# Two graph-attention layers on one core: layer 1 sums its ones column with the rows and lets a tile's projection run on into the next tile; the first part computes its score columns apart from the weights

## Chip, core and metric

The kernel runs on one core of a Trainium2 chip. The time is the device time of that core in microseconds (us), from the first to the last instruction. Three runs of the kernel before took 2431.86, 2438.90 and 2444.07 us; the median, 2438.9 us, is the number to compare with. The profile was taken in a run of 2431.86 us, and its span is 2430.1 us.

## What is computed

`x` has 3327 rows of 1024 floats, `adj` is a symmetric 0/1 matrix (int32) with ones on the diagonal and about 17 ones per row. Cut to its core, the reference is:

```python
def layer0(x):                       # 8 heads of 128
    h = (x @ W0).reshape(C, 8, 128)
    e = leaky_relu(src(h)[:, i] + dst(h)[:, j], 0.2)      # per head
    attn = softmax(where(adj, e, -inf)); out = attn @ h
    return out
def layer1(x):                       # one head
    h = x @ W1
    e = leaky_relu(h @ a1 + (h @ a2).T, 0.2)
    return relu(softmax(where(adj > 0, e, -9e15)) @ h)
x = layernorm(x + layer0(x))
x = layernorm(x + layer1(x))
```

Everything is float32 on the chip, except where a mask or a bf16 split is named.

## The kernel before

The 3327 rows are 26 tiles of 128 (`NT = 26`). The kernel has three stages, one after the other.

**First part.** For each tile: load 128 rows of `x` and of `adj`, transpose `x`, project it with `W0`, store the projected row with its score terms in device memory (`h0_d`), and turn the tile's mask into a list of edges. A tile of 128 targets has room for `EB = 5` blocks of 512 edges, and each edge has the number of the row to fetch (`idx`) and a one-hot of its target (`oh`). The score columns (8 heads, source and target) are 16 more columns beside `W0`, so one set of products gives both:

```python
ph = Phase(own, "proj", {"A": 2, "S": 1, "T": 2})          # PSUM tags and their buffers
def project(t, ht, cuts):
    for c in cuts:                                          # CUTS0 = (0, 347, 694, 1040)
        c0, c1 = CUTS0[c], CUTS0[c + 1]
        acc = bank("A", [P, c1 - c0], "mm")
        for k in range(KT):                                 # KT = 8
            nc.tensor.matmul(acc, xT[t][:, k, :], wt[:, k, c0:c1], start=k == 0, stop=k == KT - 1)
            if k % 2 == 1:
                fill()                                      # a piece of the edge list of an earlier tile
        m = min(c1, D) - c0
        nc.scalar.activation(ht[:, c0 : c0 + m], acc[:, :m], AF.Copy)
        if c == 2:
            nc.scalar.activation(sd0[:, t]..., acc[:, m:], AF.Copy)
            ...                                             # two small exponentials, then the store of ht
for k in range(KT):                                         # score columns of W0, once
    for n, av in enumerate(avs):
        pr = ph.sbuf("pr", [P, D], 4)
        (nc.vector, nc.gpsimd)[n].tensor_tensor(pr, wt[:, k, :D], av, OP.mult)
        nc.vector.tensor_reduce(wt[:, k, D + n * H : D + (n + 1) * H], ..., AX.X, OP.add)
```

Inside the edge list, a 0/1 matrix `place` sends entries to slots:

```python
nc.vector.scalar_tensor_tensor(mid, off, 1.0, end, op0=OP.mult, op1=OP.add)
nc.scalar.activation(away, self.io_q, AF.Abs, bias=mid, scale=-1.0)
...
nc.vector.tensor_scalar(place, away, deg, None, op0=OP.is_lt)
yield
xp = bank("S", [P, NG, HALF], "xp")                         # four PSUM banks at once
for b in range(EB):
    ...                                                     # 16 small products
    yield
nc.scalar.activation(oh..., xb[:, :, :, :GT], AF.Copy)      # three evictions for all four groups
...
```

**Layer 0.** For each tile, five steps gather 4 x 128 rows of `h0_d` by `idx` and sum them with weights per head. The change does not touch it.

**Layer 1.** For each tile `t`, five steps `b` gather 4 x 128 rows of `y_d` (1024 values, a one, two exponentials), build the weights `es` on VectorE, and sum on TensorE. Four products of 32 output rows each (`g = 0..3`) stand side by side in the array. The sum of the weights is a column of its own (`den`). When the tile is summed it is divided by `den`, transposed and multiplied with `W1`; that projection is a generator (`project1`) whose pieces are called by `fill()` during the next tile's steps:

```python
ph = Phase(own, "sparse", {"A": 4, "S": 2, "T": 1, "D": 1})
def project1(t, z, res):
    xT = sbuf("xT", [P, KT, P], 2)
    yield from ph.transposed(xT, z)          # two pieces: four transposes into tag "T", one copy out
    acc = [bank("S", [P, HALF], "mm") for _ in range(2)]
    for k in range(KT):
        for g in range(2):
            nc.tensor.matmul(acc[g], xT[:, k, :], wt[:, k, g * HALF : (g + 1) * HALF], ...)
        yield
    o = sbuf("z", [P, D], 3, "o")
    for g in range(2):
        nc.scalar.activation(o[:, g * HALF : (g + 1) * HALF], acc[g], AF.Relu)
    nc.vector.tensor_tensor(o, o, res, OP.add)
    ph.layer_norm([o])
    nc.sync.dma_start(out[...], o[:n])
    yield
# class Target:
def begin(self):
    self.acc = [bank("A", [P, HALF], "acc1") for _ in range(2)]
    self.den = bank("D", [P, 1], "den1")
def step(self, b):
    s = self.src.pop(b)
    nc.vector.tensor_tensor(es, R, s[:, :, D + 1 : D + 2], OP.mult)      # cut: broadcasts
    nc.vector.tensor_tensor(es, es, s[:, :, D + 2 : D + 3], OP.max)
    nc.vector.tensor_tensor(es, es, self.oh[:, b * NG : (b + 1) * NG, :], OP.mult)
    for c in range(3):
        for g in range(NG):
            to = self.den if c == 2 else self.acc[c]
            nc.tensor.matmul(to[g * GT : (g + 1) * GT, :], es[:, g, :],
                             s[:, g, c * HALF : min((c + 1) * HALF, D + 1)], start=b == 0, stop=b == EB - 1)
        if c < 2:
            fill()
def finish(self):
    nc.vector.reciprocal(ri[:, :1], self.den)
    nc.scalar.activation(z[:, :HALF], self.acc[0], AF.Copy, scale=ri[:, :1])
    nc.vector.tensor_scalar(z[:, HALF:], self.acc[1], ri[:, :1], None, op0=OP.mult)
    ...
    later.append(project1(self.t, z, res))
for t, tg in enumerate(targets):
    tg.begin()
    for b in range(EB):
        tg.step(b)
        ...                                  # fetch of the same step of the next tile
    while later:
        fill()
    tg.finish()
```

The order in the program is not the order on an engine: the tile framework's scheduler places the instructions of each engine itself when the kernel is built.

Of the kernel before, what the change touches and what calls it, by code (L numbers as in the profile page):

```python
# [26 lines left out]
def kernel(  # L27
# [48 lines left out]
    CUTS0 = (0, 347, 694, HW0)  # L76
# [58 lines left out]
    class Phase:  # L135
# [61 lines left out]
        def iota(self, shape, pattern, name, mult=0, base=0):  # L197

            raw = self.pool.tile(shape, I32, tag="iota", bufs=1, name="iota")
            nc.gpsimd.iota(raw, pattern=pattern, base=base, channel_multiplier=mult)  # L200
            dst = self.pool.tile(shape, F32, bufs=1, name=name)
            nc.vector.tensor_copy(dst, raw)
            return dst

        def edge_constants(self):
# [7 lines left out]
            self.io_q = self.iota([P, EB * P], [[2, EB * P]], "io_q", base=1)  # L213
# [17 lines left out]
        def edges(self, t, words, got):  # L231
# [32 lines left out]

            mid = sbuf("mid", [P, 1], 1)
            nc.vector.scalar_tensor_tensor(mid, off, 1.0, end, op0=OP.mult, op1=OP.add)
            away = sbuf("away", [P, EB * P], 1)
            nc.scalar.activation(away, self.io_q, AF.Abs, bias=mid, scale=-1.0)
# [5 lines left out]
            nc.vector.tensor_scalar(place, away, deg, None, op0=OP.is_lt)  # L274
# [3 lines left out]
            xp = bank("S", [P, NG, HALF], "xp")  # L278
            for b in range(EB):
                for n in range(4):  # L280
                    for g in range(NG):
                        r = slice(g * GT, (g + 1) * GT)
                        pl = place[r, b * P : (b + 1) * P]
                        to = xp[:, g, b * (GT + NX) : (b + 1) * (GT + NX)]
                        if n:
                            nc.tensor.matmul(to[:, GT:], pl, mv[r, n - 1, :], start=n == 1, stop=n == 3)
                        else:
                            nc.tensor.matmul(to[:, :GT], pl, self.local_b[r], start=True, stop=True)
                yield
            xb = xp[:, :, : EB * (GT + NX)].rearrange("p g (b c) -> p b g c", b=EB)  # L290
            nc.scalar.activation(oh.rearrange("p (b g) t -> p b g t", g=NG), xb[:, :, :, :GT], AF.Copy)
            nc.scalar.activation(xs, xb[:, :, :, GT : GT + KMAX + 1], AF.Copy)
            nc.scalar.activation(re.rearrange("p (b g) h -> p b g h", g=NG), xb[:, :, :, GT + KMAX + 1 :], AF.Copy)
            yield
# [17 lines left out]
    with ExitStack() as own:  # L312
        ph = Phase(own, "proj", {"A": 2, "S": 1, "T": 2})
        pool, bank = ph.pool, ph.bank
        xts, xT, ads = {}, {}, {}

        masks = [pool.tile([P, NP], U8, bufs=1, name=f"ad{n}") for n in range(4)]
        for ad in masks[:3]:
            nc.vector.memset(ad[:, N:], 0.0)
        nc.vector.memset(masks[3], 0.0)  # L320
        nc.vector.memset(masks[3][:, :1], 1.0)

        def load(t):
            xts[t] = ph.sbuf("x", [P, D], 3)
            load_rows(xts[t], x, t)
            ads[t] = masks[t % 3 if t < NT - 1 else 3]
            nc.gpsimd.dma_start(ads[t][: rows(t), :N], adj[t * P : t * P + rows(t), :])  # L327

        def flip(t):
            xT[t] = ph.sbuf("xT", [P, KT, P], 3)  # L330
# [27 lines left out]
        def project(t, ht, cuts):  # L358

            for c in cuts:  # L360
                c0, c1 = CUTS0[c], CUTS0[c + 1]
                acc = bank("A", [P, c1 - c0], "mm")
                for k in range(KT):
                    nc.tensor.matmul(acc, xT[t][:, k, :], wt[:, k, c0:c1], start=k == 0, stop=k == KT - 1)  # L364
                    if k % 2 == 1:
                        fill()
                m = min(c1, D) - c0
                nc.scalar.activation(ht[:, c0 : c0 + m], acc[:, :m], AF.Copy)  # L368
                if c == 2:
                    nc.scalar.activation(sd0[:, t].rearrange("p a h -> p (a h)"), acc[:, m:], AF.Copy)  # L370
                    nc.scalar.activation(ht[:, D : D + H], acc[:, m + H :], AF.Exp)
                    nc.scalar.activation(ht[:, D + H :], acc[:, m + H :], AF.Exp, scale=SLOPE)
                    nc.sync.dma_start(h0_d[t * P : (t + 1) * P, :], ht)

        load(0)

        wt = pool.tile([P, KT, HW0], F32, bufs=1, name="wt")
        for k in range(KT):
            nc.sync.dma_start(wt[:, k, :D], w0[k * P : (k + 1) * P, :])
# [16 lines left out]
        ph.edge_constants()  # L396
        for k in range(KT):
            for n, av in enumerate(avs):
                pr = ph.sbuf("pr", [P, D], 4)
                (nc.vector, nc.gpsimd)[n].tensor_tensor(pr, wt[:, k, :D], av, OP.mult)  # L400
                nc.vector.tensor_reduce(
                    wt[:, k, D + n * H : D + (n + 1) * H], pr.rearrange("p (h d) -> p h d", h=H), AX.X, OP.add
# [15 lines left out]
        hts = {}  # L418
        for t in range(NT):
# [4 lines left out]
            if t < 2:  # L424
                hts[t] = ph.sbuf("ht", [P, HW0], 3), count(t)
            if t == 0:
                project(t, hts[t][0], (0, 1))
            elif t == 1:
# [66 lines left out]
    def sparse(own):  # L495
# [221 lines left out]
        for t, tg in enumerate(targets):  # L717
# [7 lines left out]
            while later:  # L725
                fill()
# [155 lines left out]
```

## Time and profile before

| stage, us from the start | length, us | TensorE busy | VectorE busy | granted clock | DMA share |
|---|---|---|---|---|---|
| first part, 0 to 60 | 60.0 | 31.5 | 29.7 | 0.97 | 0.86 |
| first part, 60 to 560 | 500.0 | 439.6 | 399.2 | 0.95 | 0.35 |
| layer 0, 560 to 1466 | 906.0 | 554.8 | 414.6 | 0.73 | 0.85 |
| layer 1, 1530 to 2380 | 850.0 | 726.9 | 220.4 | 0.85 | 0.83 |

The rows come from the table of busy time by stretch. "Busy" is time in which an engine ran an instruction; the granted clock is the share of its full clock that TensorE got; the DMA share is the mean busy share of the 16 DMA engines. Between 1466 and 1530 the first rows of layer 1 are fetched; after 2380 the last tile is projected and normalised. In layer 1 a tile takes 34.1 us, one after the other: the reciprocal of `den` (L705) starts at 1801.34 us in one tile and at 1835.47 us in the next.

A weight load shows as PEld, a product as PE; a float32 product has two records of each. "128x512 x16" on a line of the timeline are therefore eight products of 512 columns, or two groups of four side by side.

### The profile page before, as it was taken

How to read it: one execution, taken by the hardware profiler on the slowest of the kernel's cores; microseconds unless marked ns; L12 is line 12 of the kernel's file. 1: busy time of each engine (PE TensorE's matmuls, PEld its weight loads, DVE VectorE, ACT ScalarE, POOL GpSimd, SP SyncE). 2: the span in 40 equal slices, each digit the busy share in tenths (PEclk: the TensorE clock that was granted, in tenths of full speed). 3: DMA queues.
4: the chain of work that ended last, by engine and by line, in shares of the span. 5: the costliest groups of instructions: out<-in, count | busy, mean ns of one | idle time of the engine just before them, and what ended most of it. 6: DMA issues, size and time to landing. Idle time of an engine off the chain costs nothing. (4 is left out here: it accounts for less than half of the span.)

```text
span 2430.1 us, 43110 instructions
## 1 busy us (share of the span) xinstructions
PE 1793.1 (74%) x17125; PEld 933.1 (38%) x17125; DVE 1079.2 (44%) x2883; ACT 444.5 (18%) x780; POOL 1157.1 (48%) x1139
## 2 busy tenths in 40 slices
PE   5988889992666666666666653788888888888884
PEld 3554455651434444443444441233333333333331
DVE  5987879857434444334443442222222222222221
ACT  3344442221101111011110110111111111111110
POOL 3100000005666666666666655656656566666640
PEclk9999999995677687788767766888888888888886
DMA  8444541118898888988889866889888888889860
GB/s 188 85 83 82 96 82 64 69 39 321 287 338 298 301 304 312 329 305 299 287 302 329 294 235 239 292 296 320 295 294 295 304 296 297 285 292 319 287 209 18
DMA packets 197729, 587.30 MB, mean 242 GB/s; under 512 B 41380, under 2 KB 58020, under 8 KB 197520
## 3 DMA queue, kind: packets, MB, share of 16 engines
q0 software_dynamic: 153504, 481.26, 60.3%
q1 hardware_dynamic: 44016, 103.20, 11.7%
q8 instruction: 137, 2.24, 0.4%
q14 instruction: 72, 0.59, 0.1%
HBM read 652.62 MB, written 45.42 MB: 287 GB/s over the span
## 5 line engine op out<-in xcount | busy, mean ns | idle before, releaser
L540 POOL DMA_INDIRECT src<-h_d,idx x520 | 561.9, 1081 | 317.9 <-PE acc L605 183.3
L540 POOL DMA_INDIRECT src<-y_d,idx x520 | 536.5, 1032 | 365.9 <-PE den L696 211.6
L605 PE MATMUL acc<-src,e 128*32 128x128 f32 x8320 | 528.8, 349 | 205.4 <-issue 162.6
L605 PEld LDWEIGHTS acc<-src,e 128*32 128x32 f32 x8320 | 347.2, 139 | 359.2 <-issue 304.4
L364 PE MATMUL mm<-wt,xT 128*128 128x347 f32 (+1 forms) x1248 | 426.8, 485 | 29.1 <-DMA wt<-in_L_gnn_W_dram 20.6
L696 PE MATMUL acc<-src,es 128*32 128x512 f32 x2080 | 338.5, 774 | 129.3 <-DVE es L692 94.5
L559 PE MATMUL mm<-wt,xT 128*128 128x512 f32 x832 | 389.0, 608 | 0.0
L364 PEld LDWEIGHTS mm<-wt,xT 128*128 128x128 f32 x1248 | 232.9, 198 | 144.7 <-DMA wt<-in_L_gnn_W_dram 21.8
L566 DVE TENSOR_TENSOR o<-o,res 128x1024 f32<-128x1024 f32 x26 | 31.9, 1226 | 514.3 <-ACT o L565 493.6
L559 PEld LDWEIGHTS mm<-wt,xT 128*128 128x128 f32 x832 | 148.9, 191 | 149.2 <-issue 147.7
L696 PEld LDWEIGHTS acc<-src,es 128*32 128x32 f32 x2080 | 65.0, 129 | 335.1 <-issue 215.4
L599 DVE TENSOR_TENSOR e<-ohf,w 128x1024 f32<-128x1024 f32 x130 | 159.0, 1224 | 4.8 <-PE acc L605 1.4
L327 POOL DMA_DIRECT2D ad<-in_adj_dram x26 | 14.4, 554 | 271.7 <-ACT ht L368 56.1
L620 DVE RECIPROCAL ri<-den 128x8 f32<-128x8 f32 x26 | 5.4, 208 | 280.6 <-PE acc L605 155.3
L613 PE MATMUL den<-w,ohf 128*32 128x8 f32 x1040 | 48.3, 197 | 110.2 <-DVE sg L172 66.6
L625 DVE SCALAR_TENSOR_TENSOR y<-acc,ri,y 128x128 f32<-128x128 f32 x208 | 56.2, 343 | 124.9 <-PE acc L605 85.9
L173 ACT ACT_TABLE_LOAD x50 | 64.2, 1283 | 228.5 <-DVE sg L172 205.7
L581 ACT ACTIVATE ohf<-oh 128x640 f32<-128x640 uint8 x26 | 19.2, 737 | 448.7 <-PE acc L605 231.3
L341 ACT ACTIVATE junk<-ad 128x3328 uint8<-128x3328 uint8 x26 | 77.5, 2979 | 99.1 <-DMA ad<-in_adj_dram 99.1
L613 PEld LDWEIGHTS den<-w,ohf 128*32 128x32 f32 x1040 | 39.4, 130 | 137.2 <-issue 100.2
L565 ACT ACTIVATE o<-mm 128x512 f32<-128x512 f32 x52 | 31.1, 597 | 278.9 <-PE mm L559 278.9
L154 PE MATMUL tr<-ident,z 128*128 128x128 f32 x208 | 47.0, 365 | 43.5 <-ACT z L707 41.9
(124 smaller groups left out, 1548.2 us busy)
## 6 DMA issues: line engine op xcount, KB each, us to landing
h_d<-ht SPq DMA_DIRECT2D x26, 520.0 KB
y_d<-y SPq DMA_DIRECT2D x26, 514.0 KB
res<-y_d SPq DMA_DIRECT2D x26, 512.0 KB
x<-in_x_dram SPq DMA_DIRECT2D x25, 512.0 KB
y<-in_x_dram SPq DMA_DIRECT2D x25, 512.0 KB
out_dram<-o SPq DMA_DIRECT2D x25, 512.0 KB
ad<-in_adj_dram POOLq DMA_DIRECT2D x25, 415.9 KB
src<-h_d,idx POOLq DMA_INDIRECT x520
```

Of the source, the lines that this page charges most:

```text
L154: nc.tensor.transpose(tr[:, k, :], src[:, (4 * g + k) * P : (4 * g + k + 1) * P], ident)
L173: nc.scalar.activation(sg[:, 0, :nt], sg[:, 0, :nt], AF.Sqrt)
L341: nc.scalar.activation(junk, ad, AF.Copy, accum_out=deg)
L364: nc.tensor.matmul(acc, xT[t][:, k, :], wt[:, k, c0:c1], start=k == 0, stop=k == KT - 1)
L540: nc.gpsimd.indirect_dma_start(out=s[:, g, :w], out_offset=None, in_=table[:, :], in_offset=bass.IndirectOffsetOnAxis(ap=idx[:, t, b * NG ...
L559: nc.tensor.matmul(acc[g], xT[:, k, :], wt[:, k, g * HALF : (g + 1) * HALF], start=k == 0, stop=k == KT - 1)
L566: nc.vector.tensor_tensor(o, o, res, OP.add)
L599: nc.vector.tensor_tensor(e, self.ohf[:, blk, :].unsqueeze(2).to_broadcast([P, NG, H, GT]), w.unsqueeze(3).to_broadcast([P, NG, H, GT]), O ...
L605: nc.tensor.matmul(self.acc[h // 4][g * GT : (g + 1) * GT, h % 4, :], e[:, g, h, :], s[:, g, h * DH : (h + 1) * DH], start=b == 0 and h % ...
L613: nc.tensor.matmul(self.den[g * GT : (g + 1) * GT, :], self.ohf[:, b * NG + g, :], w[:, g, :], start=b == 0, stop=b == EB - 1,)
L625: nc.vector.scalar_tensor_tensor(yh, self.acc[h // 4][:, h % 4, :], ri[:, h : h + 1], yh, op0=OP.mult, op1=OP.add)
L696: nc.tensor.matmul(to[g * GT : (g + 1) * GT, :], es[:, g, :], s[:, g, c * HALF : min((c + 1) * HALF, D + 1)], start=b == 0, stop=b == EB - 1,)
```

## The change

It does two things at once.

1. **Layer 1.** The ones column is no longer a product of its own. The 1025 columns are cut in three parts of 342, 342 and 341, each summed in a PSUM bank, so the sum of the weights comes out in the last part. And the projection of a tile is no longer finished before the tile that runs beside it is finished: the generator begins with three empty pieces, three pieces are called after each step, and the loop that called what was left ahead of `finish` is gone. This is meant to put the next tile's first products in place of the wait for the divided sums, and to save the separate product.
2. **First part.** The score columns leave `W0`. `W0` is multiplied in two halves of 512 columns; the scores come from `wa`, 32 columns wide, in eight small products, a copy and one more product (`scores`). `place` is made by two comparisons on VectorE in place of one on ScalarE and one on VectorE; the small products of the edge list go through two banks, twice, with twelve evictions in place of three; the score columns are multiplied on VectorE alone; the buffers of `adj` are cleared at each load; `xT` and `ht` have two buffers in place of three, the projection's sums four banks in place of two.

```diff
-        ph = Phase(own, "proj", {"A": 2, "S": 1, "T": 2})
+        ph = Phase(own, "proj", {"A": 4, "S": 2, "T": 2})
...
-            ads[t] = masks[t % 3 if t < NT - 1 else 3]
-            nc.gpsimd.dma_start(ads[t][: rows(t), :N], adj[t * P : t * P + rows(t), :])
+            ads[t] = ph.sbuf("ad", [P, NP], 3, dt=U8)
+            load_adj(ads[t], t)                      # a memset, then the load
...
-            nc.vector.tensor_scalar(place, away, deg, None, op0=OP.is_lt)
+            nc.vector.tensor_scalar(place, self.io_q, end, None, op0=OP.is_ge)
+            nc.vector.tensor_tensor(end0, end, deg, OP.subtract)
+            nc.vector.scalar_tensor_tensor(place, self.io_q, end0, place, op0=OP.is_ge, op1=OP.subtract)
...
+            for g0 in range(0, NG, 2):
+                xp = [bank("S", [P, EB, GT + NX], "xp") for _ in range(2)]
+                ...                                  # 40 small products, then six evictions
...
+        def scores(t, ht):
+            st = bank("T", [P, P], "st")
+            for k in range(KT):
+                g = k % NG
+                nc.tensor.matmul(st[g * GT : (g + 1) * GT, :], wa[:, k, :], xT[t][:, k, :], ...)
+            nc.scalar.activation(ss, st, AF.Copy)
+            sp = bank("T", [P, 2 * H], "sp")
+            nc.tensor.matmul(sp, ss, ph.local[:, : 2 * H], start=True, stop=True)
+            nc.vector.tensor_copy(sd0[:, t]..., sp)
+            ...                                      # the two exponentials
...
-                (nc.vector, nc.gpsimd)[n].tensor_tensor(pr, wt[:, k, :D], av, OP.mult)
+                nc.vector.tensor_tensor(pr, wt[:, k, :], av, OP.mult)
...
         def project1(t, z, res):
+            for _ in range(3):
+                yield
...
-                self.acc = [bank("A", [P, HALF], "acc1") for _ in range(2)]
-                self.den = bank("D", [P, 1], "den1")
+                self.acc = [bank(tag, [P, CUTS[1]], "acc1") for tag in "AAD"]
...
-                            to[g * GT : (g + 1) * GT, :], es[:, g, :],
-                            s[:, g, c * HALF : min((c + 1) * HALF, D + 1)], start=b == 0, stop=b == EB - 1,
+                            self.acc[c][g * GT : (g + 1) * GT, : CUTS[c + 1] - CUTS[c]], es[:, g, :],
+                            s[:, g, CUTS[c] : CUTS[c + 1]], start=b == 0, stop=b == EB - 1,
                         )
-                    if c < 2:
-                        fill()
+                for _ in range(3):
+                    fill()
...
-            while later:
-                fill()
             tg.finish()
```

## The prediction

> **What bounds the kernel now.** I read the page's slices first, then the table by stretch for the stages, then one tile of layer 1 in the timeline, then the granted clock inside that tile.
>
> ```profile
> PE   5988889992666666666666653788888888888884
> PEclk9999999995677687788767766888888888888886
> DMA  8444541118898888988889866889888888889860
> ```
>
> Nine slices of 60.8 us are the first part with TensorE full at nearly full clock. Then comes layer 0 at DMA 8 to 9 tenths, which the change leaves alone. The last 15 slices are layer 1: PE 8, clock 8, DMA 8, no engine plainly full.
>
> ```profile
> 60.00:360.00 300.00, 256.98 (x1938) 153.93 (x1937) 251.19 (x805) 127.20 (x239) 17.64 (x22) 0.94 0.47 87
> 360.00:550.00 190.00, 182.60 (x1540) 110.25 (x1538) 144.48 (x436) 53.46 (x151) 0.95 (x1) 0.99 0.16 58
> 1530.00:2380.00 850.00, 726.89 (x4008) 266.75 (x4012) 220.44 (x621) 133.33 (x195) 498.63 (x482) 0.85 0.83 286
> ```
>
> The columns are length, busy PE, PEld, DVE, ACT, POOL, then clock, DMA share, GB/s. From 60 to 360 us PE (86%) and DVE (84%) are both near their limit and hold each other up; from 360 on PE alone is (96%). Layer 1 has DVE at 26% and DMA at 83%, so by sums PE is nearest (86%), and part of that is slow clock. The timeline of one tile says why:
>
> ```profile
> 1827.89 0.60 ACT L565 ACTIVATE o<-mm 128x512 f32<-128x512 f32 x1 [0.20 <-PE mm L559]
> 1828.52 1.23 DVE L566 TENSOR_TENSOR o<-o,res 128x1024 f32<-128x1024 f32 x1 [19.88 <-ACT o L565]
> 1829.66 0.28 DVE L687 TENSOR_TENSOR es<-R,src 128x128 f32<-128x128 f32 x1
> 1831.26 0.27 DVE L692 TENSOR_TENSOR es<-es,oh 128x128 f32<-128x128 f32 x1
> 1831.59 3.64 PE L696 MATMUL acc<-src,es 128*32 128x512 f32 x16 [3.74 <-DVE es L692]
> 1836.47 1.12 PE L154 MATMUL tr<-ident,z 128*128 128x128 f32 x4 [1.17 <-ACT z L707]
> 1837.51 3.41 PE L696 MATMUL acc<-src,es 128*32 128x512 f32 x16
> 1845.25 1.92 PE L696 MATMUL acc<-src,es 128*32 128x512 f32 x16
> ```
>
> The scheduler has put the residual add (L566) and half the norm of the previous tile ahead of the weights `es` of the last step, so PE stands 3.74 us; then 1.17 us more for the divided sums. After the gap the same 16 records take 3.64 us, later 1.92: half clock. Cut at the clock's changes:
>
> ```profile
> 1827.85:1830.32 2.47, 0.00 (x1) 0.00 (x0) 1.80 (x3) 1.88 (x2) 2.17 (x2) 1.00 0.96 366
> 1830.32:1833.73 3.41, 2.14 (x12) 0.60 (x16) 2.67 (x9) 0.20 (x1) 1.29 (x2) 0.50 0.94 335
> 1833.73:1837.15 3.42, 2.25 (x19) 1.08 (x12) 1.29 (x4) 0.69 (x1) 1.26 (x2) 0.50 0.99 358
> 1837.15:1840.56 3.41, 3.41 (x19) 0.63 (x17) 2.26 (x7) 0.00 (x0) 2.79 (x3) 0.50 0.66 226
> 1840.56:1861.98 21.42, 21.42 (x121) 8.41 (x117) 0.88 (x3) 2.75 (x4) 13.24 (x14) 1.00 0.88 298
> ```
>
> Three windows of 3.41 us at 0.50, with PE busy 63%, 66% and 100% of them; only after the full one the clock rises. 7.8 busy us at half clock cost 3.9 us a tile. And 34.13 us is ten such windows: the loop has locked to them.
>
> **What the Trainium skill says.** *TensorE: Matmul & The Clock Gate*, "The HAM clock gate": the array's clock is halved or full, set by how busy it was in a free-running window of 3413 ns. The trace agrees (0.50 or 1.00, 10.24 us = 3 windows). The same page, "Architectural detail", says that ACT and DVE are strict FIFO; the trace agrees, `es` waits behind L566 with its inputs long there. *TensorEngine Tiling (Array Packing)*, "Key Properties": a change of tiling mode drains the array. The trace has about 0.2 us at each change from projection to sums (8 records of 0.427 us are 3.41, the stretch is 3.63). *PSUM — Partial Sum Buffer*, "The four PSUM rules": one product goes to one bank of 512 columns, so 1025 columns need three banks either way; no run here tests it.
>
> **The change part by part: layer 1.** The tile before, from the last projection product (1827.85) to the next tile's (1861.98): 3.74 wait + 3.70 last step + 1.18 wait + 4.97 transposes and first step + 20.54 projection and three steps = 34.13.
>
> In the built order of the changed kernel TensorE runs: last step, *first step of the next tile*, eight transposes, then projection and steps as before. VectorE still has the residual add ahead of the last step's `es`. At full clock:
> - wait for `es`: 3.74, unchanged;
> - a step: six passes of 342 columns at 0.833 ns (347 columns took 0.29 us a pass in the first part) = 1.71, against 1.88 with the ones column apart. Last step 1.71;
> - wait ahead of the first step: its last `es` operation stands behind the reciprocal on VectorE, which needs the last step's sums: 0.18 + 0.17 + 0.27 + 0.06 (before's latency, reciprocal, L692, start) = 0.7;
> - first step 1.71, in which the division is done;
> - transposes 0.66 + 0.66, but through one bank of tag T, so the second four wait for the first copy (0.69) and two hand-overs: 0.9. Sum 2.2. Before, the first step filled that wait;
> - the rest: 20.54 - 3 x 0.17 = 20.0.
>
> Sum 30.1, against 34.13 - 3.9 = 30.2 for before at full clock. So the steps save 0.85 us in five, the moved first step saves some of one wait and opens another: at full clock **almost nothing**. What may change is the slow windows. In this trace the clock rises after a window with PE busy above about 0.78, and falls after one below about 0.58 (I compared every window of the trace with the next). After the change the second slow window holds step, 0.7 wait, step: (3.41 - 0.7) / 3.41 = 0.79, just at the edge. One slow window costs up to 1.7, two about (6.8 - 1.3 - 0.7) / 2 = 2.4, three about (10.2 - 1.3 - 1.6) / 2 = 3.7. That makes 31.8, 32.5 or 33.8 us. I take 32.1: **2.0 x 25 tiles = 50 us gained**. The last tile's tail stays.
>
> DMA is no obstacle here: 0.83 x 34.13 = 28.3 us a tile.
>
> **The first part.** TensorE: 24 products of 347 at 0.58 = 13.9 us become 16 of 512 at 0.855 = 13.7, plus eight score products of 128 columns four abreast (0.43) and one small: +0.3. VectorE per tile: a second comparison of 640 values (0.82 as in L299), one difference, one copy of scores and one memset (0.15 each), less `mid` (0.16): +1.1, on some 17 of 21 us. ScalarE: twelve small evictions in place of three, less the `away` pass (0.84): about +1, in slack. Once: eight multiplications of 1.2 us move from GpSimd to VectorE, +8 at 40 to 80 us, where TensorE must wait for the score weights. Sum on VectorE 26 x 1.1 + 8 = 37; in the last 190 us (DVE 76%) some 8 of it hide. New waits: the score product waits for a copy on ScalarE, five users a tile share two T banks, the small products share two S banks: I put 7. **First part: +36 us**.
>
> Together 2438.9 - 50 + 36 = 2425.
>
> **The rivals.**
> 1. *Layer 1 stays locked at 34.13 us.* If the wait ahead of the first step is 0.8 and not 0.7, the second window stays under the edge, three windows are slow, and ten windows a tile is again a stable beat. For it: the wait for `es` is untouched, and the present lock. Then nothing is gained and the time is 2475.
> 2. *Layer 1 finds nine windows, 30.72 us.* For it: the second slow window is fuller than before. Gain 85, time 2390. Against: DMA would be at 0.92.
> 3. *The first part costs nothing, or much more.* Four banks A free TensorE from waits for evictions (ACT waits 92 us for `adj` loads from 60 to 560, and PE behind it), which could pay for all of the 36: time 2390. Or the shared T banks tie PE to VectorE's queue twice a tile: another 2 us in each, time 2475.
> 4. *DMA becomes the bound of layer 1.* At 32 us a tile the share is 0.88; it would have to lose efficiency. Least likely.
>
> **Range and chances.** Layer 1 -85 to 0, first part 0 to +85, largely independent: about 40 us to either side of 2425 as one deviation, so 2375 to 2480 eight times in ten. Faster by over 2% (below 2390) needs both parts on the good side: 0.22. Slower by over 2% (above 2488) needs the lock and a bad first part: 0.10. The rest 0.68.
>
> **What would show it.** Reciprocals of layer 1 32 us apart on average and not evenly, with one or two slow windows; 34.13 even means rival 1, 30.72 rival 2. The wait ahead of the last step still 3.7 us and named for `es`; a wait of 0.9 between the two groups of transposes; a step 1.7 us at full clock. The flag after the first part at about 585 to 600 us and not 548. If the wait ahead of the last step is gone, or layer 0 moves from its 33.6 us a tile, I have read the order wrongly.

## Result, and the profile after

The changed kernel takes 2472.96 us (median of four runs, 2468.75 to 2475.6) against 2441.48 us for the kernel before on the same chip: a ratio of 1.0135, with a 95% interval of 1.0102 to 1.0167. That is 31.5 us slower. I had forecast 2425 us, 14 us faster. The first part cost what I forecast; layer 1 gave next to nothing of the 50 us.

These are the slices of the changed kernel, to be read beside those of before.

```profile
PE   6787888995566666665665563687778787887874
PEclk9898889998678778778877775799999999899997
DMA  6443453213998888898888885888889888888860
```

In the last 14 slices, which are layer 1, the granted clock has gone from 8 to 9 tenths, as was hoped, but PE has gone down from 8 to between 7 and 8: the time that the clock gave back is idle time of TensorE. The table by stretch has it in numbers (length, busy PE, PEld, DVE, ACT, POOL, clock, DMA share, GB/s):

```profile
60.00:360.00 300.00, 242.32 (x1765) 116.17 (x1765) 236.53 (x781) 119.41 (x301) 10.03 (x19) 0.89 0.46 80
...
1575.00:2424.00 849.00, 680.46 (x4019) 264.44 (x4018) 228.20 (x642) 129.84 (x195) 495.54 (x482) 0.92 0.84 287
```

From 60 to 360 us neither TensorE (242 us) nor VectorE (237 us) is as near its limit as before (257 and 251): they wait more for each other and for ScalarE. Layer 1 is as long as before (849 against 850 us) with 46 us less of TensorE. The reciprocals of its tiles are 34.0 us apart on average (the 22 tiles of the table below), unevenly, from 31.0 to 35.7. The timeline of one tile shows where the idle time sits, first TensorE, then VectorE, then two of the gathers that GpSimd issues at that moment:

```profile
2012.22 2.69 PE L693 MATMUL acc<-src,es 128*32 128x342 f32 x24 [3.74 <-DVE es L690]
2015.52 2.47 PE L693 MATMUL acc<-src,es 128*32 128x342 f32 x24 [0.61 <-DVE es L690]
2017.93 0.66 PE L153 MATMUL tr<-ident,z 128*128 128x128 f32 x4
2021.63 0.66 PE L153 MATMUL tr<-ident,z 128*128 128x128 f32 x4 [3.04 <-DVE xT L158]
```

```profile
2015.04 0.17 DVE L702 RECIPROCAL ri<-acc 128x1 f32<-128x1 f32 x1 [0.76 <-PE acc L693]
2015.39 1.04 DVE L709 TENSOR_SCALAR z<-acc,ri 128x340 f32<-128x340 f32 x2
2020.88 0.69 DVE L158 COPY xT<-tr 128x512 f32<-128x512 f32 x1 [4.45 <-remote]
```

```profile
2017.73 0.99 POOL L537 DMA_INDIRECT src<-y_d,idx  x1 [0.30 <-issue]
2019.02 0.99 POOL L537 DMA_INDIRECT src<-y_d,idx  x1 [0.30 <-PE tr L153]
```

The first two waits, 3.74 and 0.61 us, are the ones forecast (3.74 and 0.7). The third is not: 3.04 us between the two groups of transposes, where I had 0.9. The first four end at 2017.93 + 0.66 = 2018.59, and VectorE, which has nothing else to do, begins to copy them only at 2020.88. The copy waits for TensorE's signal alone. Its releaser is printed as "remote", which means that the page found no local event that fits: by the records TensorE had long finished. The trace also records the signals, that is, the updates of the semaphore that VectorE waits on. The one that releases the copy stands at 2020.86, so it came 2.3 us later than the recorded end.

I measured this lag, from the recorded end of the first four transposes to the start of the copy, in every tile. In the kernel before it is 0.04 us in all 26, as in the tile of the prediction, where the four transposes end at 1836.47 + 1.12 = 1837.59:

```profile
1837.62 0.69 DVE L159 COPY xT<-tr 128x512 f32<-128x512 f32 x1 [0.86 <-PE tr L154]
```

In the changed kernel it is 1.62 us on average, over 0.3 in 22 of 26, and 2.79 at most.

The other runs are compared by the same account, in us a tile, as the mean of 22 tiles. Busy and idle columns add up to the tile within 0.3 us; the half-clock column is part of the busy time (half of it is lost).

| layer 1 of | tile | TensorE busy | of it at half clock | idle ahead of steps or projection | idle ahead of transposes |
|---|---|---|---|---|---|
| kernel before | 34.13 | 29.17 | 7.69 | 3.77 | 1.14 |
| forecast for the change | 32.1 | 26.8 | 4.0 | 4.44 | 0.9 |
| changed kernel | 34.03 | 27.08 | 4.16 | 4.34 | 2.59 |
| e2_layer1 | 34.19 | 27.30 | 4.53 | 4.24 | 2.64 |
| e3_split | 33.04 | 28.04 | 5.84 | 3.89 | 1.06 |
| e4_pin_l1 | 30.87 | 27.22 | 4.04 | 0.07 | 3.44 |
| e5_ones | 33.40 | 28.63 | 6.73 | 3.74 | 0.98 |
| e6_runon | 33.26 | 28.25 | 6.38 | 3.81 | 1.14 |
| e7_hold_split | 34.31 | 27.53 | 4.93 | 6.64 | 0.00 |
| e8_even | 33.43 | 27.43 | 4.80 | 5.91 | 0.00 |
| e9_two_banks | 33.82 | 27.00 | 3.73 | 6.79 | 0.00 |
| e10_weave | 30.30 | 26.61 | 2.53 | 0.08 | 3.39 |
| e13_weave_wide | 31.11 | 26.91 | 2.95 | 0.04 | 3.88 |
| e15_weave_six | 31.64 | 27.09 | 2.41 | 0.46 | 3.98 |
| e16_order_gather | 35.00 | 27.45 | 4.88 | 4.55 | 2.98 |
| e17_order_rows | 32.23 | 27.02 | 3.98 | 4.40 | 0.78 |
| e18_order_pool | 32.25 | 27.04 | 4.02 | 4.40 | 0.78 |

The forecast's busy time is its 30.1 at full clock less its three waits (3.74, 0.7, 0.9), plus the 2.0 us for slow windows. Every term was right within 0.3 us except the last column.

### The profile page after: what moved, and what is told of

Its sections match the earlier page's. It is cut to its first block, busy times and chain, and to the rows that moved or that the text cites. A ratio compares the mean times of both kernels' runs of the same rounds, so it can differ in the third digit from the quotient of the medians.

```text
span 2471.3 us, 43475 instructions
## 1 busy us (share of the span) xinstructions
PE 1770.2 (72%) x17177; PEld 878.4 (36%) x17177; DVE 1114.5 (45%) x2991; ACT 447.5 (18%) x962; POOL 1127.0 (46%) x1132
## 5 line engine op out<-in xcount | busy, mean ns | idle before, releaser
L604 PE MATMUL acc<-src,e 128*32 128x128 f32 x8320 | 523.2, 341 | 207.1 <-issue 164.4
L604 PEld LDWEIGHTS acc<-src,e 128*32 128x32 f32 x8320 | 339.3, 136 | 361.7 <-issue 308.1
L425 PE MATMUL mm<-wt,xT 128*128 128x512 f32 x832 | 423.1, 647 | 12.2 <-DMA wt<-in_L_gnn_W_dram 12.2
L693 PE MATMUL acc<-src,es 128*32 128x342 f32 (+1 forms) x3120 | 299.1, 515 | 145.0 <-DVE es L690 120.2
L558 PE MATMUL mm<-wt,xT 128*128 128x512 f32 x832 | 394.5, 619 | 0.0
L558 PEld LDWEIGHTS mm<-wt,xT 128*128 128x128 f32 x832 | 155.1, 196 | 199.7 <-issue 199.7
L693 PEld LDWEIGHTS acc<-src,es 128*32 128x32 f32 x3120 | 97.9, 120 | 353.0 <-issue 181.2
L425 PEld LDWEIGHTS mm<-wt,xT 128*128 128x128 f32 x832 | 157.7, 204 | 177.2 <-issue 154.7
L153 PE MATMUL tr<-ident,z 128*128 128x128 f32 x208 | 38.5, 310 | 74.1 <-issue 31.9
L156 ACT ACTIVATE xT<-tr 128x512 f32<-128x512 f32 x78 | 46.6, 599 | 201.0 <-PE tr L153 145.6
```

The costliest lines, as they stand in the source:

```text
L153: nc.tensor.transpose(tr[:, k, :], src[:, (4 * g + k) * P : (4 * g + k + 1) * P], ident)
L156: nc.scalar.activation(part, tr, AF.Copy)
L425: nc.tensor.matmul(acc[g], xT[t][:, k, :], wt[:, k, g * HALF : (g + 1) * HALF], start=k == 0, stop=k == KT - 1)
L604: nc.tensor.matmul(self.acc[h // 4][g * GT : (g + 1) * GT, h % 4, :], e[:, g, h, :], s[:, g, h * DH : (h + 1) * DH], start=b == 0 and h % ...
L693: nc.tensor.matmul(self.acc[c][g * GT : (g + 1) * GT, : CUTS[c + 1] - CUTS[c]], es[:, g, :], s[:, g, CUTS[c] : CUTS[c + 1]], start=b == 0, ...
```

## Experiments

Two hints to the scheduler are used below. `keep(i)` says that instruction `i` is not issued ahead of what the program put before it on its engine; `after(i)` that what follows on that engine is not issued ahead of `i`. Neither adds a wait for data.

### The halves apart: e1_first, e2_layer1

e1_first is the kernel before with only the first part's lines of the diff, e2_layer1 with only layer 1's.

> The first part of the changed kernel alone, layer 1 as before. My theory: the first part costs about +40 us and layer 1 nothing, so about 2480 us, 1.016 of before, the last count at about 573 us and not 546, and layer 1 at 34.1 us a tile. Rival: the halves depend on each other (the changed layer 1 pays or costs something that the comparison of the two traces hides); then this run is more than 10 us away from 2480.

> The changed layer 1 alone, first part as before. My theory: layer 1 gains next to nothing, 0 to 5 us in all, ratio 0.997 to 1.0; 34.1 us a tile, 3.7 us ahead of the last step for the weights es, and 2.7 to 3 us between the first and the second four transposes. My forecast was 50 us of gain, that is 2389 us.

e1_first: 2475.1 us, ratio 1.0148 (1.0125 to 1.0170), or 36 us slower. e2_layer1: 2436.6 us, ratio 0.9989 (0.9981 to 0.9997), or 2.7 us faster. Together 33 us slower, against 31.5 measured for both, so no dependence of the halves shows. Layer 1's 50 us are gone within layer 1.

### Fold and run-on apart: e5_ones, e6_runon

```diff
 # e5_ones: three banks; the calls of fill() and the loop ahead of finish() as before
-  self.acc = [bank("A", ...) for _ in range(2)]; self.den = bank("D", [P, 1], "den1")
+  self.acc = [bank(tag, [P, CUTS[1]], "acc1") for tag in "AAD"]
 # e6_runon: three empty pieces, three fill() after a step, no loop ahead of finish(); den as before
```

> The kernel before with the ones column folded into three banks of 342 columns, everything else as before: the projection is finished before the division, and no empty pieces. Theory A (the fold saves 0.17 us a step at full clock, 0.85 us a tile, but the loop is held to ten clock windows): 34.1 us a tile and within 5 us of before. Rival B: the fold alone moves the slow windows, since a step becomes shorter and TensorE less busy in the window that decides: more than 10 us to either side.

> The kernel before with the projection running on into the next tile, the ones column still a product of its own. Theory A (run-on moves the first step ahead of the transposes and opens a wait between the transposes in its place): within 10 us of before, and the late start of the copy out of bank T, 2 us after the records end the transposes, is there without the fold as well. Rival B: the late start belongs to the products of 342 columns; then here the copy starts 0.04 us after the transposes, as in the kernel before, and the tile is about 2 us shorter, 50 us in all.

e5_ones: ratio 0.9935 (0.9915 to 0.9955), 16 us gained. e6_runon: 0.9888 (0.9861 to 0.9916), 27 us gained. Each alone gains, both together gain 2.7. Theory A of both missed. Rival B of e5_ones held: the fold alone moved the slow windows (6.73 us a tile at half clock against 7.69) and more than 10 us. Rival B of e6_runon was right on the copy, which starts 0.04 us after the transposes in every tile of both runs, but not on the amount. The reason is in the built order. With either alone, the scheduler leaves the four transposes ahead of the next tile's first step, as before, and the other four behind it; the table shows the old waits (3.7 and 1.0 to 1.1) and less half clock. Only both together move the first step ahead of all eight transposes, and only then the new gap opens. "Run-on" as I read it in the source took place only in the combination.

### A second bank for the transposes: e3_split, e7_hold_split, e9_two_banks

```diff
 # e3_split
-  tr = self.bank("T", [P, 4, P], "tr")
+  tr = self.bank("ST"[g], [P, 4, P], "tr")
 # e7_hold_split: also, all transposes after(last product of the next tile's first step)
 # e9_two_banks: also, VectorE held to the order of e2_layer1 around the reciprocal
```

> As e2_layer1, and the first four transposes go to a bank of tag S, so that the second four no longer wait for the copy out of the only bank T. Theory A (the single bank T is what ate the forecast gain): the 2.7 to 3 us between the groups shrink to under 1, a tile takes 32 us, about 50 us less than e2_layer1. Rival B (TensorE itself ends the first four transposes late, and the time between the groups is work of TensorE that the records place too early): the gap moves behind the second four and the time stays within 10 us of e2_layer1.

> As e2_layer1, the first four transposes in a bank of tag S as in e3_split, but all eight held behind the first step of the next tile on TensorE, which is the order of the changed kernel (in e3_split the scheduler had moved that step back behind seven transposes). Theory A (the single bank T ate the gain): no gap between the two groups of transposes, a tile 2 us shorter than the 34.0 of e2_layer1, 50 us in all. Rival B: TensorE is late as such; the gap moves to the first products of the projection, and the time stays within 10 us of e2_layer1.

> As e2_layer1, the first four transposes in a bank of tag S, and now VectorE and TensorE both held to the order of e2_layer1 (in e7_hold_split the norm had moved ahead of the weights es of the next tile's first step, and that wait took the place of the gap). Theory A (the wait for the only bank is what was mis-sized): the 2.6 us a tile between the transposes go and nothing takes their place; the tile is 1.7 to 2.6 us shorter than 34.2, 45 to 65 us in all. Theory B (TensorE signals the end of the first four about 2 us after the records end them, and the first product of the projection needs their copy in any case): only the 0.66 us of the second four are hidden, the idle time moves ahead of the projection, 10 to 20 us in all.

e3_split gained 1.1% (0.9891, 0.9853 to 0.9929), but it is no test: with the second bank the scheduler put seven transposes back ahead of the first step. e7_hold_split held that order and gained nothing (1.0011, 0.9998 to 1.0024), but VectorE now ran the norm ahead of the first step's `es`, and TensorE stood 3.07 us there. Its copy was mostly on time, 0.04 us after the transposes in 19 of 26 tiles. e9_two_banks holds both engines, and gains 0.3% (0.9972, 0.9958 to 0.9986), 7 us. Its timeline:

```profile
1952.05 1.09 PE L154 MATMUL tr<-ident,z 128*128 128x128 f32 x8
1956.06 5.40 PE L568 MATMUL mm<-wt,xT 128*128 128x512 f32 x8 [2.91 <-issue]
```

```profile
1955.31 0.69 DVE L159 COPY xT<-tr 128x512 f32<-128x512 f32 x1 [4.56 <-remote]
```

The eight transposes now run in one go and end at 1953.14, the copy still begins at 1955.31, and the gap of 2.9 us stands ahead of the projection. That is theory B in kind, with 7 us in place of its 10 to 20: the single bank was the place where the wait showed, not its cause. The cause is the late signal.

### What makes the signal late: e11_lone, e14_lone_more

Both leave out all attention and run units of constant data in the instruction shapes of layer 1; the edit is what the expectations tell.

> No attention at all, the output is meaningless: ten phases of eight units on constant data. A unit is four projection steps, a step of 4 x 32 rows, four projection steps, then n steps in a row, four transposes, a copy on VectorE, four transposes through the same bank, a copy on ScalarE. Phases: n = 2 without transfers; n = 2 with plain loads; n = 2 with gathers; n = 1 without; n = 1 with gathers; n = 2 with two passes of 512 columns, without and with gathers; n = 4 without and with gathers; n = 0 with gathers. Read is the time from the recorded end of the first four transposes to the start of the copy. If it is TensorE's own density that makes the signal late, 0.04 us for n = 0 and 1 and up to 2 us for n = 2 and 4, with and without transfers. If it is the transfers, 0.04 in every phase without them and 0.7 to 2.8 with them, n = 0 too perhaps. If it is the form of 342 columns, none in the phases of 512.

> No attention, the output is meaningless: units as in e11_lone, with six or twelve plain loads of 512 KB a unit beside the gathers, to bring the transfers to the share of the kernel. Phases of eight units, two quiet units after each: gathers alone (0.87 us late in e11_lone); gathers of 16 columns[...]; six loads and no gathers; twelve loads and no gathers; gathers and six loads; the same with steps of 512 columns; the same with one step; the same with passes of 170 columns; passes of 170 columns without transfers; the same with no step. If descriptors make it late: 0.87 in phase two, 0.1 in three and four. If the load of the transfers: 0.1 in phase two, 0.9 or more in four and five, up to 2 us in five. If the number of short instructions: grows from 512 over 341 to 170 columns, and is there in phase nine without transfers.

| phase | lag of the copy, us | where |
|---|---|---|
| two or four steps of 341 columns, no transfers | 0.04 to 0.09 | e11 |
| two steps, plain loads (twelve: DMA share 0.77) | 0.09 | e11, e14 |
| two steps, gathers | 0.80 to 0.89 | e11, e14 |
| four steps, gathers | 0.85 to 1.08 | e11 |
| two steps, gathers of 16 columns (DMA share 0.02) | 4.07 to 4.12 | e14 |
| two steps, gathers and six loads (0.88) | 0.84 to 1.58 | e14 |
| two steps of 512 columns, gathers and six loads (0.94) | 0.10 to 0.15 | e14 |
| one step or none, gathers and six loads | 0.09 | e14 |
| two steps in passes of 170 columns, gathers and six loads | 3.56 to 6.35 | e14 |
| passes of 170 columns, no transfers | 0.09 | e14 |

(Where two kinds of phase meet, the last two units already run beside the transfers of the next; they are left out there, as is the first unit of a phase with no step.) Two units of e11_lone, the first without transfers and the second with gathers, TensorE each:

```profile
98.29 3.65 PE L96 MATMUL acc<-fixed,es 128*32 128x341 f32 x48
101.88 0.66 PE L121 MATMUL tr<-ident,z 128*128 128x128 f32 x4
103.37 0.66 PE L121 MATMUL tr<-ident,z 128*128 128x128 f32 x4 [0.84 <-DVE xT L126]
```

```profile
467.07 3.66 PE L96 MATMUL acc<-src,es 128*32 128x341 f32 x48
470.66 0.66 PE L121 MATMUL tr<-ident,z 128*128 128x128 f32 x4
472.92 0.66 PE L121 MATMUL tr<-ident,z 128*128 128x128 f32 x4 [1.60 <-DVE xT L126]
```

Without transfers the gap through one bank is 0.84 us, which is my 0.9. With gathers it is 1.60. Neither the load on the transfers nor TensorE's density does it alone: it takes gathers, even ones that move almost nothing, together with a run of short products, and it is longer the shorter the products are (512, 341, 170 columns). GpSimd in the second of these units:

```profile
469.26 0.99 POOL L84 DMA_INDIRECT src<-in_x_dram,row  x1 [12.16 <-PE acc L96]
470.55 0.99 POOL L84 DMA_INDIRECT src<-in_x_dram,row  x1 [0.31 <-PE acc L96]
471.85 0.99 POOL L84 DMA_INDIRECT src<-in_x_dram,row  x1 [0.30 <-issue]
```

The end of a step releases a buffer, and so GpSimd issues its next gathers just while the second step and the transposes run. In none of these runs is the signal late where that does not coincide. The row "one step or none" is therefore no test of the number of products: with one step the gathers begin only 0.32 us after the transposes do, and with none there are no gathers at that moment. The rows of 512, 341 and 170 columns are one, since gathers run there in all three. It is not the number of signals: in the last 4 us up to the end of the transposes TensorE sends 17 of them with 512 columns, which are on time, and 15 with 341, which are late. Why gathers of 16 columns make it later than full ones (4.1 us against 0.8 to 0.9) is open.

### The same in the kernel: e16_order_gather, e17_order_rows, e18_order_pool

All three have the order of the changed layer 1 on TensorE and VectorE, held; they differ in how the rows are fetched, and in e17 and e18 the sums are of other rows than the reference's.

```diff
-  self.src[b] = gather(y_d, HW, self.t, b)                       # e16
+  for g in range(NG): nc.sync.dma_start(s[:, g, :HW], y_d[r : r + P, :])    # e17; nc.gpsimd in e18
```

> The control: first part as before, layer 1 of the changed kernel with its order on TensorE and VectorE held, rows by gathers. Expected as e2_layer1: 34 us a tile, 2.6 us between the two groups of transposes, the copy out of bank T up to 2.8 us after the recorded end of the first four; within 10 us of before.

> As e16_order_gather, but layer 1 takes 4 x 128 rows in sequence by plain loads on the SyncE queue in place of the gathers (as many bytes, other rows, so the sums mean nothing). Theory A (gathers make TensorE's signals late, and that is the term I mis-sized): the copy starts 0.04 us after the transposes, 0.9 us between the groups, and the tile takes what I forecast, 31.8 to 32.5 us, some 45 us less than e16. Theory B (something else in the kernel): 2.6 us stay between the groups.

> As e17_order_rows, the plain loads issued by GpSimd. If it is the queue or the engine that matters, the signal is late as with gathers and the tile takes 34 us; if it is the single descriptor of every row in a gather, it is on time and the tile is that of e17.

The tile takes 35.00 us with gathers and 32.23 and 32.25 with plain loads. (e16_order_gather is slower than e2_layer1 by 0.8 us a tile, more than I expected: 1.0097, 1.0073 to 1.0121. I did not follow up what its held order costs; it is the control for the other two. Their total times, 2364.8 and 2366.1 us, are some 104 us under its own, but only about 69 of these are the tiles of layer 1: the first reciprocal of layer 1 also comes about 36 us earlier without gathers.) One tile of e17_order_rows, TensorE, then VectorE:

```profile
1894.11 3.58 PE L722 MATMUL acc<-src,es 128*32 128x342 f32 x24 [3.86 <-DVE es L711]
1898.28 1.93 PE L722 MATMUL acc<-src,es 128*32 128x342 f32 x24 [0.58 <-DVE es L711]
1900.14 0.66 PE L154 MATMUL tr<-ident,z 128*128 128x128 f32 x4
1901.58 0.65 PE L154 MATMUL tr<-ident,z 128*128 128x128 f32 x4 [0.79 <-DVE xT L159]
```

```profile
1900.83 0.69 DVE L159 COPY xT<-tr 128x512 f32<-128x512 f32 x1 [1.65 <-PE tr L154]
```

and one of e16_order_gather:

```profile
1932.26 0.66 PE L154 MATMUL tr<-ident,z 128*128 128x128 f32 x4
1935.97 0.66 PE L154 MATMUL tr<-ident,z 128*128 128x128 f32 x4 [3.06 <-DVE xT L159]
```

```profile
1935.23 0.69 DVE L159 COPY xT<-tr 128x512 f32<-128x512 f32 x1 [4.48 <-remote]
```

Without gathers the copy starts 0.03 us after the transposes, its releaser has a name again, the gap is 0.79, and the tile is the 32.1 us of my forecast within 0.2. The mean lag over all tiles is 2.01 us in e16 and 0.04 in e17 and e18. e18 shows that it is not GpSimd as issuer that matters: its plain loads leave the signal on time, although GpSimd issues them at the same moment (1893.85 and 1896.35 us in a tile whose transposes start at 1896.01).

### Taking the waits away: e4_pin_l1, e8_even, e10_weave, e13_weave_wide, e15_weave_six

```diff
 # e4_pin_l1 (on e2_layer1): es of the last step no longer stands behind the residual add
-  nc.vector.tensor_tensor(o, o, res, OP.add)
+  keep(nc.vector.tensor_tensor(o, o, res, OP.add))
 # e8_even (on e7_hold_split): es of the next tile's first step ahead of the reciprocal;
 #   residual add and norm behind the second step's es, one tile later; no empty pieces
+  targets[t + 1].weigh(0)
   tg.finish()                                    # keep(nc.vector.reciprocal(...))
+  if b == 1 and tails: tail1()                   # keep(residual add), norm, store
 # e10_weave (on e8_even): TensorE in program order; in front of finish() two pieces of the
 #   previous projection, behind it the eight transposes, then the next first step
-  nc.tensor.matmul(...)
+  keep(nc.tensor.matmul(...))
-  for _ in range(3): fill()
+  for _ in range((2, 2, 1, 1, 3)[b]): fill()     # e15_weave_six: (1, 2, 1, 1, 4)
 # e13_weave_wide (on e10_weave): two passes of 512 columns, the ones column apart
+  CUT1 = (0, HALF, D, D + 1)
```

> As e2_layer1, with the residual add of the projected tile held behind the weights es of the last step in VectorE's order; the work is the same. Theory A: the 3.7 us ahead of the last step go, TensorE stays at full clock, a tile takes 30 us or less, about 100 us less than e2_layer1. Rival B: the loop keeps a beat of ten windows of 3.41 us and the time comes back in another wait (the first step of the next tile, or the transposes): within 20 us of e2_layer1. Rival C: the transfers become the bound, DMA share over 0.95, at 29 to 30 us a tile.

> First part as before, layer 1 as in e7_hold_split and two things more: the weights es of the next tile's first step are built ahead of the division, and the residual add and norm of a tile come behind the second step's es of the tile after next. No sum is left out. If the three waits (es of the last step, es of the first step, bank T) are what holds the tile, TensorE needs 26 to 27 us a tile at full clock and the transfers (0.83 of 34.1 = 28.3 us) become the bound: 28.5 to 29.5 us a tile, some 120 us less than before, 2315 us, DMA share 0.95 or more, clock 0.95 or more. Rival: the loop settles on nine windows, 30.7 us, as e4_pin_l1 nearly did (30.9): 2355 us.

> Layer 1 of the same sums in a held order on TensorE: last step, the last two pieces of the projection of the tile before (four products of 512, 3.4 us, over the division), eight transposes in two banks, first step of the next tile (over the copies), then the projection. The weights es of the first step are built ahead of the division, residual add and norm after the second step. First part as before. Theory A: no wait of the tile is left, two steps never follow each other, the late signals stop; TensorE needs 25 us a tile at full clock and the transfers bound it at 28.5 to 29.5 us: about 2315 us. Rival: late signals come whenever transfers are dense, whatever the order; then a wait of 1 to 3 us stays at the transposes and the tile takes 31 us or more, 2355 us.

> As e10_weave, the steps again in two passes of 512 columns and the ones column apart, as in the kernel before. Theory A (many short instructions make the signal late): the wait of 3.4 us ahead of the transposes shrinks under 1 us although a step is 0.2 us longer; the tile takes 28.5 to 29 us against 30.3, 30 to 40 us less than e10_weave. Rival B (the transfers make it late whatever the columns): the wait stays at 3 us or more and the time is that of e10_weave within 10 us.

> As e10_weave, six products of the projection in place of four between the last step and the transposes. If the late signal is a fixed 2 us, the wait of 3.4 us ahead of the transposes falls by 1.7 and the tile takes 28.6 us, 40 us less in all. Rival: the other steps now stand closer together, the signal is later by as much, and the time stays within 10 us of e10_weave.

e4_pin_l1 is the smallest edit of all, one line on top of e2_layer1, and gains 3.2% (0.9677, 0.9656 to 0.9697): the 3.7 us ahead of the last step are gone, and 30.9 us a tile remain. Theory A held for that wait, but the gain over e2_layer1 is 77 us and not 100: TensorE's order came out anew, with the transposes ahead of the next first step, and they wait 3.44 us, most often for a reciprocal whose signal is late. Rivals B and C missed (DMA share 0.91). e8_even, which was to take all three waits away, gains only 0.9% (0.9906, 0.9887 to 0.9926): 33.4 us a tile, where I had named 28.5 to 29.5 or 30.7. Its order puts the last step and the next first step side by side; the first step's third pass then waits 1.91 us for the only bank D, and the late signal leaves 3.98 us ahead of the projection. e10_weave gains 4.0% (0.9605, 0.9588 to 0.9622), 2351.75 us against 2449.28: faster than both kernels, but not the 2315 of theory A. Its rival came nearer (31 us a tile or more and 2355; measured 30.3), though not its reason: in e17_order_rows the transfers are dense too (share 0.93) and the signal is on time. TensorE and VectorE there:

```profile
1937.82 3.70 PE L559 MATMUL mm<-wt,xT 128*128 128x512 f32 x8
1944.85 1.20 PE L154 MATMUL tr<-ident,z 128*128 128x128 f32 x8 [3.33 <-ACT z L720]
```

```profile
1943.20 0.17 DVE L714 RECIPROCAL ri<-acc 128x1 f32<-128x1 f32 x1 [9.11 <-remote]
```

The last step ends at 1937.9 by the records, and the reciprocal starts 5.3 us later: the four products of 512 columns cover 3.6 us (1937.89 to 1941.52) of a signal that came later still. TensorE itself went on: the records of these products begin every 0.43 us from 1938.35 on. So it is the signal that is late and not the work, as far as the records tell, and it does not take two steps in a row: here none follow each other. e13_weave_wide (0.9645, 0.9629 to 0.9661) does not shorten that wait (3.88 us), although steps of 512 columns were on time on constant data: rival B held. With the ones column apart a step has as many products as before, 12, so this run does not test their number; that the late signal needs products of 342 columns it rules out. e15_weave_six (0.9732, 0.9674 to 0.9791) puts two more products over it and loses: 3.98 us, and by the ratios some 31 us more in all than e10_weave, so its rival missed as well. In both, theory A failed. No order that I tried hides the late signal while the gathers are issued at that moment, and I tried none that moves the gathers.

### One piece of the first part: e12_place

```diff
-  nc.scalar.activation(away, self.io_q, AF.Abs, bias=mid, scale=-1.0); nc.vector.tensor_scalar(place, away, deg, None, op0=OP.is_lt)
+  nc.vector.tensor_scalar(place, self.io_q, end, None, op0=OP.is_ge)   # and end0 = end - deg
+  nc.vector.scalar_tensor_tensor(place, self.io_q, end0, place, op0=OP.is_ge, op1=OP.subtract)
```

> The kernel before with one piece of the changed first part: place made by two comparisons on VectorE and no pass on ScalarE. My sum had 0.82 + 0.15 - 0.16 = 0.8 us a tile for it, 21 us over 26 tiles, of which some 5 hide in the last third: +15 us, ratio 1.006. Rival: it hides wholly, since ScalarE loses a pass of 0.84 us and VectorE waited for it: within 4 us. Then the 36 us of e1_first come from other parts, the small products and their evictions before all.

It is faster: 0.997 (0.9957 to 0.9984), 7 us; both the theory (15 us slower) and the rival (within 4 us) missed. These are two groups of 60 to 540 us, the kernel before first:

```profile
L270 DVE CAST mv<-pack 128x41 bf16<-128x41 f32 x75 | 13.6, 182 | 32.4 <-ACT pack L262 32.0
```

```profile
L265 DVE CAST mv<-pack 128x41 bf16<-128x41 f32 x75 | 13.6, 181 | 12.6 <-ACT pack L262 12.0
```

The second comparison costs VectorE 22 us, but VectorE waited 20 us less for ScalarE. The wait that fell is for the exponential of L262, which presumably comes sooner when the pass is gone; that was not tested. My term of +21 us for this piece was right as work and wrong as time.

## Why the prediction was right or wrong, point by point

- **The first part, +36 us:** right as a total (36 us in e1_first; the flag, the value computed after the first part that chooses how to go on, at 589.9 us, inside the 585 to 600 named). Its breakdown was not. I made it of VectorE's extra work with 7 us of new waits. One such piece alone gains time (e12_place), and e1_first has new waits that add up to far more than 7: over 60 to 570 us, VectorE stands 39.1 us for the score product (`sd` on `sp`), 30.0 us with `place` behind the small products of the tile before, and TensorE 32.9 us for their evictions. How much of these is on the path was not separated. The number was right partly by luck.
- **Layer 1, steps and waits for `es`:** right. 3.74 us ahead of the last step, 0.61 ahead of the first (0.7), projection and steps as summed.
- **Slow windows:** right. 4.16 us a tile at half clock cost 2.1 us, where I took 2.0; one or two windows a tile, and the lock at ten windows is broken.
- **The wait between the two groups of transposes, 0.9 us:** this is the step that failed. It was worked out as a copy of 0.69 us and two hand-overs, which leaves some 0.1 us for each. It measures 2.59 us, because TensorE's signal to the copy comes 1.62 us late on average. The sum is then 32.1 + 1.7 = 33.8 us a tile, against 34.0; 1.7 us in 25 tiles are 42 of the 45 us missed in layer 1. The hand-over is short without gathers: 0.84 us in e11_lone, 0.78 in e17_order_rows, where the whole tile is 32.23 us and not the 35.00 of e16_order_gather. Gathers at that moment are not new: in the tile of the prediction GpSimd issues them at 1835.58, 1836.87 and 1838.17 us, beside the transposes of 1836.47, and the lag is 0.04. New is that two steps run right ahead of the transposes; in the kernel before, the transposes came behind one step and a wait of 1.1 us. The clock is not the difference, since e6_runon has tiles with the four transposes at full clock (0.66 us) and a lag of 0.04. I took a short hand-over into an order in which it does not hold. The runs show that it fails with gathers and not with plain loads; they don't settle why, nor the exact condition, since e10_weave has a late signal without two steps in a row.
- **Two readings of the trace of before** that the sum rests on. The lower edge of the clock rule, 0.58, did not hold in the changed kernel: there 47 windows at full clock with TensorE busy less than that, down to 0.41, were followed by another at full clock. In before itself none of 91 rises came after a window under 0.78 and none of 92 falls after one above 0.60, but 7 and 11 windows beyond these edges changed nothing. And the 0.2 us at a change from projection to sums are for the change there and the one back, about 0.1 each (records begin 0.53 and 0.52 us apart in place of 0.43).
- **Rivals.** Rival 1 named nearly the time (2475) for the wrong reason: the tile is not locked and the wait ahead of the first step is under 0.7. Rivals 2, 3 and 4 did not come: no tile of nine windows, a first part at the 36 us forecast, and with plain loads a DMA share of 0.93 at 32.2 us a tile, the time that TensorE's work and waits add up to.
- **What I did not see** is that the wait that mattered most was untouched by the change: holding one residual add back (e4_pin_l1) is worth 77 us on top of e2_layer1.

## What to carry to other kernels

A hand-over from TensorE is short only in the conditions in which it was seen. If a change puts it right behind a long run of short products, and gathers are issued at that moment, allow 2 us or more; a consumer whose releaser the profile calls "remote", on an idle engine, is the mark of it. Read the built order of an engine and not the source: two edits that gained 16 and 27 us alone gained 3 together, because only together they changed that order. And look first at what stands ahead of the critical operand in an in-order queue, since moving that cost one line here and was worth half as much again as the 50 us hoped for in layer 1.

## What the runs showed of the hardware that was not expected

- TensorE's signals come late when gathers and a run of short products coincide: 0.80 to 0.89 us with two steps of 341 columns, 3.56 to 6.35 with passes of 170 (and six loads), 4.07 to 4.12 with gathers that move almost nothing, up to 2.79 in the changed kernel; with two steps of 512 columns 0.10 to 0.15. In the tile of the changed kernel shown, the last products and the transposes end by the records between 2017.99 and 2018.59, and their signals come at 2018.67, 2018.72, 2019.40, 2020.14 and 2020.86, mostly some 0.7 us apart. What delays them is open. It is no error of the trace alone: the tiles of e16 and e17 take 35.00 and 32.23 us.
- Plain loads do not do this, at a DMA share of 0.77 on constant data and 0.93 in the kernel, nor when GpSimd issues them (e18_order_pool, 0.04 us).
- A second comparison of 640 values on VectorE in place of a pass on ScalarE cost VectorE 22 us in e12_place, and its waits for ScalarE fell by 20 us; the kernel was 7 us faster.
